# A decoder layer on one core: the first batch alone through its recurrence, context tiles behind the first heads, and four banks for the last product

## The chip, the cores and the metric

The kernel runs on one core of one Trainium2 chip. A core has TensorE (PE, the matrix engine, with its weight loads shown apart as PEld), VectorE (DVE), ScalarE (ACT), GpSimd (POOL) and SyncE (SP, which here only issues DMAs). Each engine works through its own instructions in order and waits on semaphores for the others. The metric is the device time of one execution in microseconds (us); a smaller number is better. Runs are compared by their median.

## The reference, cut to what matters

One decoder layer in 32-bit floats over x of shape (16, 256, 256), 16 batches of 256 tokens, with a context of 77 rows a batch:

```python
# 1. a recurrence over the tokens of each batch
h = x @ in_w.T + in_b                               # 512 channels
h = silu(depthwise_conv4(h) + conv_b)
xp = h @ xp_w.T + xp_b                              # 32 columns
a = exp(-exp(xp[..., :16]));  b = silu(xp[..., 16:]) * sum(h, -1)
state_t = state_{t-1} * a_t + b_t
x = layernorm(x + states @ out_w.T + out_b)
# 2. attention of the 256 tokens (as latents) over 77 context rows and themselves
xn = layernorm(ctx) * g_media + b_media;  ln = layernorm(x) * g_lat + b_lat
q = ln @ Wq + bq;  k, v = split(concat([xn, ln]) @ Wkv + bkv)   # 8 heads of 128
x = layernorm(x + softmax(q k / sqrt(128)) v @ Wo + bo)
# 3. eight experts, top 2 by token, at most 512 tokens each
x = layernorm(x + experts(x))
```

## The kernel before, in words

**Stages.** The kernel has an opening, a loop over 128 heads (16 batches of 8), and an expert part. The loop over heads is a software pipeline: for each head `head_kq` makes keys and queries (pk, pq), `head_softmax` the scores s, their maximum nm, the exponentials p and the normalised pn, `head_turn` the transposes ptt one head later, `head_out` the product po two heads later. Other work is hung on heads: `steps[b, h]`, filled by `at(...)`, runs after the head's keys and queries; `late_steps`, filled by `behind(...)`, after its transposes.

**The recurrence.** `rec_in(pr, c)` does one of four chunks of 128 channels for a pair of batches (512 tokens): two matmuls into a bank ph (L290), ACT copies it with the bias into hp (L293), whose first three columns POOL clears (L292, a buffer pair `bufs=2`), DVE makes the convolution cv in four instructions (L297, L299), ACT a tanh (L302) and DVE the activation hs (L303). For later pairs POOL sums hs over the chunks (L305). `rec_state` makes px and the sums sg by matmuls whose results take 32 partitions for each member (L319, L331); for the first pair its two members stand twice in the 128 partitions. Then come zb (L339), the decays on ACT (L341, L342), a permuting matmul pp (L344), and on DVE bs and the scan ys (L347 to L351). `rec_add` multiplies ys by the output weights (py, L363) and adds x (L369); `rec_out` normalises (L148, with a power on POOL, L134), `prep_norm` scales to zl (L425), `prep_keys` transposes zl and writes kvt (L437, L439), and `prep_values` makes v in seven products (L477) with weight sums wsum, which `weight_sums` makes on DVE (L448 to L451).

**The context.** The 16 x 77 context rows are ten tiles of 128 rows. `context(t)` normalises a tile, transposes it (pt, L389), writes kvc (L391), multiplies by the V half of wkv in two halves of two matmuls (pvc, L405), copies them out (DVE L413, ACT L415) and stores them to DRAM (L416), from where `prep_values` reads each batch's 77 rows. In the opening all ten tiles are called: 0 and 1 between the chunks, 2 to 4 between the steps of the first pair, and 5 to 9 after the values of batch 0.

**Banks.** PSUM has two banks "mm", which rotate between most users, one each of "pk", "pq", "pa" and "po", and a pair "s". The context's pvc use pk, pq, pa and po in turn.

**What sets the order.** A layer below the kernel orders each engine's instructions when the program is built, from the order in which the code calls them and its own estimate of their costs; the order on each engine is then fixed. Loads go out on two queues, SP's and ACT's, in the order of issue, and eight semaphores are used in turn for them: an issue waits until the earlier DMA with the same semaphore has landed.

**The last expert.** `second_product` multiplies four slots of 128 rows (pf, L996) into the two "mm" banks; for the last expert DVE adds each with its weight to y (L1004), where the gathered other halves (L985) are already added, and `finish` normalises and scatters.

Of the kernel before, what the change touches and what calls it, by code (L numbers as in the profile page):

```python
# [38 lines left out]
def decoder_layer(  # L39
# [152 lines left out]
    def load_xT(pr):  # L192

        xTs[pr] = aw.tile([P, DC, PT], F32, tag="xT", name=f"xT{pr}")
        nc.sync.dma_start(xTs[pr], xT[:, pr * PT : (pr + 1) * PT].rearrange("(c p) t -> p c t", p=P))
# [9 lines left out]
    nc.sync.dma_start(inw, in_wT.rearrange("(c p) f -> p c f", p=P))  # L205
    load_xT(0)
    for dst, src in ((inb, in_b), (cw, conv_w), (cb, conv_b), (gm, g_media), (bm, b_media)):
        nc.scalar.dma_start(dst, src)
    NCT = -(-B * M // P)

# [3 lines left out]
    ctx_flat = ctx_in.rearrange("b m d -> (b m) d")  # L214
    ctxs = []
    for t0, t1 in ((0, 1), (1, 5), (5, NCT - 1), (NCT - 1, NCT)):
        c = b2.tile([P, t1 - t0, D], F32, tag="v" if t1 - t0 == 4 else "ctx", name=f"ctx{t0}")
        rows = ctx_rows(t0)
        nc.sync.dma_start(
            c[0:rows, 0 : t1 - t0, :], ctx_flat[t0 * P : t0 * P + rows * (t1 - t0), :].rearrange("(t p) d -> p t d", p=rows)  # L220
        )
        ctxs += [c[:, i, :] for i in range(t1 - t0)]

    xpw = aw.tile([P, NI, 2 * NST], F32, tag="xpw", name="xpw")
    nc.sync.dma_start(xpw, xp_wT.rearrange("(c p) s -> p c s", p=P))
    half = aw.tile([P, 2 * NST], F32, tag="half", name="half")
    G.memset(half, 0.5)
# [4 lines left out]
    for g in range(0, P, 2 * NST):  # L232
        nc.sync.dma_start(xpb[g : g + 2 * NST], xp_b)
        nc.sync.dma_start(outw[g : g + NST], out_wT)
        nc.sync.dma_start(outw[g + NST : g + NST + 1], out_b)
# [7 lines left out]
    wkv_d = wkv.rearrange("(c p) f -> p c f", p=P)  # L243
    nc.sync.dma_start(wkv_s[:, :, INNER:], wkv_d[:, :, INNER:])
    load_x(0)
    load_x(1)
    for dst, src in ((gl, g_lat), (bl, b_lat), (bq_s, bq), (bkv_s, bkv)):
        nc.sync.dma_start(dst, src)
    nc.sync.dma_start(wkv_s[:, :, 0:INNER], wkv_d[:, :, 0:INNER])
    nc.sync.dma_start(wq_s, wq.rearrange("(c p) f -> p c f", p=P))  # L250
# [7 lines left out]
    def load_rest():  # L258
        nc.sync.dma_start(wo_s, wo.rearrange("(h p) f -> p h f", p=P))
        nc.sync.dma_start(bo_s, bo.broadcast_to([P, D]))  # L260
        nc.sync.dma_start(emb_s, embT.rearrange("(c p) e -> p c e", p=P))
    zero = wpool.tile([P, DX], F32, tag="zero", name="zero")
# [17 lines left out]
    hss, sums, yss, xs, stats = {}, {}, {}, {}, {}  # L280

    def rec_in(pr, c):

        if c == 0:
            hss[pr] = aw.tile([P, NI, PT], F32, tag="hs", bufs=2, name=f"hs{pr}")
            if pr > 0:
                sums[pr] = aw.tile([P, PT], F32, tag="sums", bufs=2, name=f"sums{pr}")
        ph = bank(f"ph{pr}_{c}")
        for k in range(DC):
            T.matmul(ph, lhsT=inw[:, k, c * P : (c + 1) * P], rhs=xTs[pr][:, k, :], start=(k == 0), stop=(k == DC - 1))  # L290
        hp = a2.tile([P, PB, KC - 1 + S], F32, tag="hp", name=f"hp{pr}_{c}")
        G.memset(hp[:, :, 0 : KC - 1], 0.0)  # L292
        A.activation(  # L293
            hp[:, :, KC - 1 :], ph.rearrange("p (b s) -> p b s", b=PB), AF.Identity, bias=inb[:, c : c + 1]
        )
        cv = a2.tile([P, PB, S], F32, tag="cv", name=f"cv{pr}_{c}")
        V.tensor_scalar(cv, hp[:, :, 0:S], cw[:, c, 0:1], cb[:, c : c + 1], ALU.mult, ALU.add)  # L297
        for k in range(1, KC):
            V.scalar_tensor_tensor(cv, hp[:, :, k : k + S], cw[:, c, k : k + 1], cv, ALU.mult, ALU.add)  # L299
        z = cv.rearrange("p b s -> p (b s)")  # L300
        th = a2.tile([P, PT], F32, tag="th", name=f"th{pr}_{c}")
        A.activation(th, z, AF.Tanh)  # L302
        V.scalar_tensor_tensor(hss[pr][:, c, :], th, 1.0, z, ALU.add, ALU.mult)  # L303
        if c > 0 and pr > 0:
            G.tensor_tensor(sums[pr], hss[pr][:, 0, :] if c == 1 else sums[pr], hss[pr][:, c, :], ALU.add)  # L305

    def rec_state(first, last):

        n = last - first + 1
        members = [first + g % n for g in range(4)]  # L310
        rows = [slice(g * 2 * NST, (g + 1) * 2 * NST) for g in range(4)]

        def tokens(b):
            return slice(b % PB * S, (b % PB + 1) * S)

        px = bank(f"px{first}")
        for c in range(NI):
            for b, r in zip(members, rows):
                T.matmul(  # L319
                    px[r, 0:S],  # L320
                    lhsT=xpw[:, c, :],
                    rhs=hss[b // PB][:, c, tokens(b)],
                    start=(c == 0),
                    stop=(c == NI - 1),
                )

        sg = bank(f"sg{first}")
        parts = [sums[b // PB] for b in members] if first else None
        for c in range(1 if first else NI):
            for g, (b, r) in enumerate(zip(members, rows)):  # L330
                T.matmul(  # L331
                    sg[r, 0:S],
                    lhsT=half,
                    rhs=parts[g][:, tokens(b)] if first else hss[0][:, c, tokens(b)],
                    start=(c == 0),
                    stop=(first > 0 or c == NI - 1),
                )
        zb = aw.tile([P, S], F32, tag="zb", name=f"zb{first}")
        V.tensor_scalar(zb, px[:, 0:S], xpb, None, ALU.add)  # L339
        dec = aw.tile([P, S], F32, tag="dec", name=f"dec{first}")  # L340
        A.activation(dec, zb, AF.Exp)  # L341
        A.activation(dec, dec, AF.Exp, scale=-1.0)  # L342
        pp = bank(f"pp{first}")
        T.matmul(pp[:, 0:S], lhsT=perm, rhs=zb, start=True, stop=True)  # L344
        bs = aw.tile([P, S], F32, tag="bs", name=f"bs{first}")
        A.activation(bs, pp[:, 0:S], AF.Tanh, scale=0.5)
        V.scalar_tensor_tensor(bs, bs, 1.0, pp[:, 0:S], ALU.add, ALU.mult)  # L347
        V.tensor_tensor(bs, bs, sg[:, 0:S], ALU.mult)
        ys = a2.tile([P, S], F32, tag="ys", name=f"ys{first}")
        V.tensor_tensor_scan(ys, dec, bs, 0.0, ALU.mult, ALU.add)  # L350
        V.tensor_scalar(ys, ys, one_row, None, ALU.add)  # L351
        for b, r in zip(members[0:n], rows):
            yss[b] = ys[r, :], outw[r, :]
# [3 lines left out]
    def rec_add(b):  # L357

        pys = [bank(f"py{b + i}") for i in range(PB)]
        for h in range(2):  # L360
            for i in range(PB):
                ys, w = yss[b + i]
                T.matmul(  # L363
                    pys[i][:, h * D : (h + 1) * D], lhsT=ys[:, h * P : (h + 1) * P], rhs=w, start=True, stop=True
                )
        for i in range(PB):
# [15 lines left out]
    def context(t):  # L382
# [3 lines left out]
        layernorm(zc, zc, 1, rows, f"c{t}")  # L386
        pt = bank(f"pt{t}")
# [10 lines left out]
        if t % 2 == 0:  # L398
            stages[t // 2] = b2.tile([P, 2, INNER], F32, tag="ot", name=f"vc{t}")
        vc = stages[t // 2][:, t % 2, :]  # L400
        for half in range(2):
            f0 = half * 512
            pv = bank(f"pvc{t}_{half}", ("pk", "pq", "pa", "po")[(2 * t + half) % 4], 1)
# [8 lines left out]
            if half == 0:  # L412
                V.tensor_copy(vc[0:rows, f0 : f0 + 512], pv[0:rows])  # L413
            else:
                A.copy(vc[0:rows, f0 : f0 + 512], pv[0:rows])  # L415
        nc.sync.dma_start(vc_d[t * P : t * P + rows, :], vc[0:rows, :])  # L416
# [27 lines left out]
    def weight_sums():  # L444
# [3 lines left out]
        V.tensor_tensor(t(0), w(0, 1), w(0, 0), ALU.subtract)  # L448
        V.tensor_tensor(t(1), w(1, 1), w(0, 1), ALU.subtract)
        V.tensor_tensor(t(2), w(1, 1), t(0), ALU.subtract)  # L450
        V.tensor_tensor(t(3), w(1, 0), t(2), ALU.subtract)  # L451
# [328 lines left out]

    for h in range(H):
        at(0, h, clear, h)
    at(1, 0, clear, H)
    for b in range(B):
# [11 lines left out]
        if new_pair:  # L796
# [4 lines left out]
            at(b, 1, rec_add, nb)  # L801
# [5 lines left out]
            for n, h in enumerate((4, 6, 7)):  # L807
                at(b, h, prep_values, nb, n, False)
                behind(b, h, prep_values, nb, n, True)
        elif nb < B:  # L810
# [7 lines left out]
    at(0, 0, load_xT, 1)  # L818
    for c in range(NI):
        at(0, 4 + c, rec_in, 1, c)  # L820
    for nb in range(4, B, 4):
# [6 lines left out]
        for c, h in enumerate((3, 4, 5, 7)):  # L828
            at(nb - 2, h, rec_in, pr + 1, c)

    rec_in(0, 0)
    rec_in(0, 1)
    context(0)
    rec_in(0, 2)
    rec_in(0, 3)
    context(1)
    rec_state(0, 1)
    context(2)
    context(3)
    rec_add(0)  # L840
    rec_out(0)
    prep_norm(0)
    prep_keys(0)
    context(4)
    rec_out(1)
# [5 lines left out]
    for t in range(5, NCT):  # L851
        context(t)
# [134 lines left out]
    def second_product(e, it):  # L987
# [5 lines left out]
        for s in range(SLOTS[e][2]):  # L993
            po = bank(f"pf{e}_{s}")
# [184 lines left out]
```

## Time and profile before

| what | us |
|---|---|
| median of 3 runs | 1200.22 (1199.39 to 1200.71) |
| the profiled execution | 1201.09 |
| its span, first to last instruction | 1199.3 |
| PE busy in the span | 1152.6 (96%) |
| DVE busy | 748.6 (62%) |
| ACT busy | 485.4 (40%) |
| POOL busy | 312.3 (26%) |

The page says how long each engine was busy, in 40 slices of the span and as groups of instructions by line. A line of the timeline gives start, time, engine, line, operation, what is written and read, and in brackets how long the engine was idle before it and what ended that. Engine time that overlaps other work does not add to the span, so the shares of busy time do not by themselves say what sets the end.

### The profile page before, as it was taken

The numbers are of one execution on the slowest core, as the hardware profiler recorded it, in microseconds if no ns is written. First come the engines' busy times: TensorE is split into PE (matmuls) and PEld (weight loads), VectorE is DVE, ScalarE is ACT, GpSimd is POOL, SyncE is SP. The second block draws the span as 40 slices with busy tenths as digits, with TensorE's granted clock in tenths as the row PEclk, the third lists the DMA queues.
The fourth block names the chain that finished last, engine by engine and source line by source line (L and its number), as shares of the span: only waits on it lengthen the run. The fifth ranks groups of instructions, "written<-read, shape, count | busy, mean of one in ns | idle before, by whom it ended". The sixth has DMA issues, their size and how long they took to land. (4 is left out here: it accounts for less than half of the span.)

```text
span 1199.3 us, 15750 instructions
## 1 busy us (share of the span) xinstructions
PE 1152.6 (96%) x5134; PEld 827.8 (69%) x5134; DVE 748.6 (62%) x2226; ACT 485.4 (40%) x1273; POOL 312.3 (26%) x560
## 2 busy tenths in 40 slices
PE   6789999999999999999999999999999999999996
PEld 2337676767777767767777777677777778876664
DVE  5535768596646765874658576756465645666665
ACT  2125434444344434443435343534343433423331
POOL 2200132222221332222213222232122211225554
PEclk8899999999999999999999999999999999999999
DMA  6760001001000110010000000010001000125762
GB/s 207 226 188 11 19 20 37 28 10 56 18 29 9 35 36 23 9 46 18 15 10 23 29 21 9 4 29 4 20 14 45 14 9 3 30 92 171 182 182 85
DMA packets 45402, 60.37 MB, mean 50 GB/s; under 512 B 7813, under 2 KB 35438, under 8 KB 45320
## 3 DMA queue, kind: packets, MB, share of 16 engines
q1 hardware_dynamic: 38552, 50.13, 13.6%
q0 software_dynamic: 6048, 9.22, 3.1%
q8 instruction: 41, 0.67, 0.2%
q14 instruction: 41, 0.34, 0.1%
q10 hardware_dynamic: 720, 0.01, 0.0%
HBM read 36.07 MB, written 30.78 MB: 56 GB/s over the span
## 5 line engine op out<-in xcount | busy, mean ns | idle before, releaser
L564 PE MATMUL po<-ptt,v 128*128 128x256 f32 (+1 forms) x768 | 190.0, 382 | 6.3 <-DVE ptt L552 6.3
L564 PEld LDWEIGHTS po<-ptt,v 128*128 128x128 f32 (+1 forms) x768 | 142.7, 190 | 58.7 <-issue 25.7
L529 DVE TENSOR_REDUCE nm<-s 128x2 f32<-128x666 f32 x128 | 108.3, 846 | 117.1 <-PE s L527 117.1
L512 PE MATMUL pk<-kvt,wkv_s 128*128 128x333 f32 x512 | 164.9, 444 | 0.0
L527 PE MATMUL s<-kt,qt 128*128 128x333 f32 x512 | 164.3, 442 | 0.0
L572 ACT ACTIVATE ot<-po,bkv_s 128x256 f32<-128x256 f32 x128 | 60.8, 475 | 218.9 <-PE po L564 218.7
L533 ACT ACTIVATE p<-s,nm 128x333 f32<-128x333 f32 x256 | 135.4, 535 | 33.7 <-DVE nm L529 32.5
L517 PE MATMUL pq<-kvt,wq_s 128*128 128x256 f32 x512 | 131.2, 378 | 0.0
L512 PEld LDWEIGHTS pk<-kvt,wkv_s 128*128 128x128 f32 x512 | 91.1, 191 | 45.0 <-issue 22.0
L527 PEld LDWEIGHTS s<-kt,qt 128*128 128x128 f32 x512 | 96.4, 188 | 31.3 <-ACT qt L519 0.5
L517 PEld LDWEIGHTS pq<-kvt,wq_s 128*128 128x128 f32 x512 | 96.7, 189 | 30.2
L582 PE MATMUL pw<-wo_s,ot 128*128 128x256 f32 x512 | 115.8, 379 | 0.0
L553 ACT COPY ptt<-pb 77x256 f32<-77x256 f32 x128 | 47.1, 368 | 168.2 <-PE pb L550 168.2
L582 PEld LDWEIGHTS pw<-wo_s,ot 128*128 128x128 f32 x512 | 97.0, 190 | 13.2
L538 DVE TENSOR_SCALAR pn<-p,rs 128x333 f32<-128x333 f32 x256 | 97.8, 416 | 3.8
L760 POOL DMA_INDIRECT xg<-xs,sidx x64 | 66.4, 1038 | 88.7 <-DVE sidx L757 68.0
L550 PEld LDWEIGHTS pa<-ident,pn 128*128 128x128 f32 x512 | 63.6, 141 | 34.8 <-DVE pn L538 6.8
L552 DVE COPY ptt<-pa 128x512 f32<-128x512 f32 x128 | 87.1, 680 | 0.6 <-PE pa L550 0.6
L596 POOL TENSOR_TENSOR xb<-xs,bo_s 128x256 f32<-128x256 f32 x30 | 19.9, 683 | 244.1 <-DVE yb L598 244.1
L550 PE MATMUL pa<-ident,pn 128*128 128x128 f32 x512 | 78.3, 274 | 2.6 <-DVE pn L538 2.6
L514 ACT ACTIVATE kt<-pk,bkv_s 128x333 f32<-128x333 f32 x128 | 69.0, 539 | 19.9 <-PE pk L512 19.6
L299 DVE SCALAR_TENSOR_TENSOR cv<-hp,cw,cv 128x512 f32<-128x512 f32 x96 | 71.8, 751 | 1.9
(231 smaller groups left out, 1670.0 us busy)
## 6 DMA issues: line engine op xcount, KB each, us to landing
v<-vc SPq DMA_DIRECT2D x16, 308.0 KB
vc<-vc SPq DMA_DIRECT2D x9, 512.0 KB
xg<-zero SPq DMA_DIRECT2D x34, 131.0 KB
xe<-xg SPq DMA_DIRECT2D x8, 524.0 KB
xT<-in_xT SPq DMA_DIRECT2D x8, 512.0 KB
xt<-in_x_in SPq DMA_DIRECT2D x16, 256.0 KB
out<-o SPq DMA_DIRECT2D x16, 256.0 KB
w<-in_w1T SPq DMA_DIRECT2D x8, 512.0 KB
```

Of the source, the lines that this page charges most:

```text
L299: V.scalar_tensor_tensor(cv, hp[:, :, k : k + S], cw[:, c, k : k + 1], cv, ALU.mult, ALU.add)
L512: T.matmul(pk[:, 0:J], lhsT=wkv_s[:, k, f], rhs=kvt[:, k, :], start=(k == 0), stop=(k == DC - 1))
L514: A.activation(kt, pk[:, 0:J], AF.Identity, bias=bkv_s[:, h : h + 1])
L517: T.matmul(pq[:, 0:S], lhsT=wq_s[:, k, f], rhs=kvt[:, k, 0:S], start=(k == 0), stop=(k == DC - 1))
L527: T.matmul(s[:, ic, 0:J], lhsT=qt[:, ic * P : (ic + 1) * P], rhs=kt, start=True, stop=True)
L529: V.tensor_reduce(nm, s[:, :, 0:J], AX.X, ALU.max, negate=True)
L533: A.activation(p[:, ic, :], s[:, ic, 0:J], AF.Exp, bias=nm[:, ic : ic + 1], accum_out=sm[:, ic : ic + 1])
L538: V.tensor_scalar(pn[:, ic, :], p[:, ic, :], rs[:, ic : ic + 1], None, ALU.mult)
L550: T.transpose(dst[0:jn, c0 : c0 + P], pn[:, ic, j0 : j0 + jn], ident)
L552: turned = V.tensor_copy(ptt[:, 0:2, :], pt01.rearrange("p (j i) -> p j i", j=2))
L564: T.matmul(po[:, 0:S], lhsT=vs[b][0:jn, jc, h * DH : (h + 1) * DH], rhs=ptt[0:jn, jc, :], start=(jc == 0), stop=(jc == 2),)
L582: T.matmul(pws[b][:, i * D : (i + 1) * D], lhsT=ot[:, h, i * P : (i + 1) * P], rhs=wo_s[:, h, :], start=(h == 0), stop=(h == H - 1),)
```

## The change

- `load_xT` and `rec_in` can take one batch of the first pair; before the heads only batch 0 goes through the recurrence (256 columns, one member in `rec_state`, which now repeats no members). Batch 1's chunks are called at heads 0 and 1, its `rec_state` at head 2, `rec_add` and `rec_out` at head 3, keys at head 4, values at heads 5, 6 and 7.
- The context is split: five tiles are normalised together (`context_norm`) and called between the steps of batch 0; tiles 5 to 9 run behind heads 0 to 4, with pt and pvc in the "mm" banks and each half stored by itself. The middle tiles are loaded into the second hs buffer; the first tiles' pt take the "s" pair.
- The loads are issued in another order: half of xT, inw in two halves, the first five tiles and the V half of wkv come first; the recurrence's small weights go to ACT's queue, and their copies for the other members after the opening.
- The four weight sums go from DVE to POOL.
- The chunks of the second pair of each four batches are called at heads 2, 3, 5, 6 instead of 3, 4, 5, 7.
- The last expert's third and fourth slots of `second_product` take the banks "pk" and "pq".

```diff
+    load_xT(0, 0)
+    nc.sync.dma_start(inw[:, :, 0 : DI // 2], inw_d[:, :, 0 : DI // 2])
+    nc.sync.dma_start(inw[:, :, DI // 2 :], inw_d[:, :, DI // 2 :])
+    load_ctx(ctx_ends[0], 0, 1)
+    load_ctx(ctx_most, 1, 5)
+    nc.sync.dma_start(wkv_s[:, :, INNER:], wkv_d[:, :, INNER:])
...
+    load_x(0)
+    nc.sync.dma_start(gl, g_lat)
+    nc.sync.dma_start(bl, b_lat)
+    nc.sync.dma_start(wkv_s[:, :, 0:INNER], wkv_d[:, :, 0:INNER])
...
+    def rec_in(pr, c, i=None):
+        a, n = (0, PB) if i is None else (i, 1)
+        cols = slice(a * S, (a + n) * S)
+        ph = bank(f"ph{pr}_{c}")[:, 0 : n * S]
...
     def rec_state(first, last):
-        n = last - first + 1
-        members = [first + g % n for g in range(4)]
+        members = range(first, last + 1)
...
+    def context_norm(t):
+        zc = ctxs[t].unsqueeze(1)
+        layernorm(zc, zc, 1, ctx_rows(t), f"c{t}")
...
+    def context(t, first):
+        if not first:
+            context_norm(t)
+        if first:
+            pt = ps.tile([P, 2, 512], F32, tag="s", bufs=1, name=f"pt{t}")[:, t % 2, :]
+        else:
+            pt = bank(f"pt{t}")
...
+            if first:
...
+                pv = bank(f"pvc{t}_{half}", ("pk", "pq", "pa", "po")[(2 * t + half) % 4], 1)
+            else:
+                vc = b1.tile([P, 512], F32, tag=("xb", "x2")[half], name=f"vc{t}_{half}")
+                pv = bank(f"pvc{t}_{half}")
...
-        V.tensor_tensor(t(0), w(0, 1), w(0, 0), ALU.subtract)
+        G.tensor_tensor(t(0), w(0, 1), w(0, 0), ALU.subtract)
...
+        elif b == 0:
+            for h in range(2):
+                at(0, h, rec_in, 0, 2 * h, 1)
+                at(0, h, rec_in, 0, 2 * h + 1, 1)
+            at(0, 2, load_xT, 1)
+            at(0, 2, rec_state, 1, 1)
+            at(0, 3, rec_add, 1, 1)
+            at(0, 3, rec_out, 1)
+            at(0, 4, prep_norm, 1)
+            at(0, 4, prep_keys, 1)
+            at(0, 4, prep_sums, 1)
+            for n, h in enumerate((5, 6, 7)):
+                at(0, h, prep_values, 1, n, False)
+                behind(0, h, prep_values, 1, n, True)
+            for h in range(NCT - FIRST_CTX):
+                behind(0, h, context, FIRST_CTX + h, False)
...
-        for c, h in enumerate((3, 4, 5, 7)):
+        for c, h in enumerate((2, 3, 5, 6)):
             at(nb - 2, h, rec_in, pr + 1, c)
...
+    for c in range(NI):
+        rec_in(0, c, 0)
+    for t in range(FIRST_CTX):
+        context_norm(t)
+    context(0, True)
+    rec_state(0, 0)
+    context(1, True)
+    rec_add(0, 1)
+    context(2, True)
     rec_out(0)
     prep_norm(0)
+    context(3, True)
     prep_keys(0)
-    context(4)
-    rec_out(1)
+    context(4, True)
     wparts = weight_sums()
     prep_sums(0)
...
-    for t in range(5, NCT):
-        context(t)
...
-            po = bank(f"pf{e}_{s}")
+            po = bank(f"pf{e}_{s}") if e < LAST or s < 2 else bank(f"pf{e}_{s}", ("pk", "pq")[s - 2], 1)
```

## The prediction

> **What bounds the kernel now.** I read the page's slices first, then the busy time by stretches of 10 us, then TensorE's timeline of the opening, then the waits of the DMA queue. The slices and stretches say that there are two regimes.
>
> ```profile
> PE   6789999999999999999999999999999999999996
> 20.00:30.00 10.00, 9.54 (x23) 3.71 (x24) 7.01 (x12) 2.79 (x5) 0.95 (x3) 0.66 0.45 181
> 40.00:50.00 10.00, 5.67 (x19) 2.39 (x17) 4.81 (x16) 1.17 (x2) 1.18 (x4) 0.89 0.64 209
> 50.00:60.00 10.00, 6.83 (x14) 3.18 (x15) 6.04 (x22) 0.81 (x2) 7.55 (x19) 0.60 0.74 215
> 100.00:110.00 10.00, 10.00 (x49) 7.91 (x49) 4.25 (x10) 5.16 (x15) 0.00 (x0) 1.00 0.00 0
> ```
>
> Columns of a stretch: length, busy time of PE, its weight loads, DVE, ACT, POOL, then the granted clock. From about 90 us on TensorE is full, so a microsecond of its work costs a microsecond. Before that it is not: over 0 to 90 us the stretches sum to 67.6 us busy, 22.4 idle, and twice the clock is down (0.66, 0.60). The timeline shows what the idle time waits for.
>
> ```profile
> 6.26 5.66 PE L290 MATMUL ph<-xT,inw 128*128 128x512 f32 x8 [6.26 <-DMA xT<-in_xT]
> 21.99 9.78 PE L405 MATMUL pvc<-wkv_s,kvc 128*128 128x512 f32 x16
> 37.47 7.13 PE L405 MATMUL pvc<-wkv_s,kvc 128*128 128x512 f32 x16
> 44.54 1.13 PE L363 MATMUL py<-outw,ys 32*128 32x256 f32 x8
> 52.18 1.45 PE L437 MATMUL pt<-ident,zl 128*128 128x128 f32 x4 [6.51 <-DVE zl L425]
> 82.41 7.13 PE L405 MATMUL pvc<-wkv_s,kvc 128*128 128x512 f32 x16 [0.68 <-ACT kvc L391]
> 89.38 1.28 PE L512 MATMUL pk<-kvt,wkv_s 128*128 128x333 f32 x4
> ```
>
> The first batch's recurrence is one chain: ph, convolution on DVE (from 13.49 us, last hs at 31.98), zb 33.27, ys ready 38.07, py only at 44.54 because context tiles 2 and 3 stand ahead of it in TensorE's queue, the add at 45.70, zl done at about 52, kvt at 55.2. The first head (pk) starts at 89.38, after five more context tiles.
>
> **The loads.** TensorE's start halves its operands: before, 1 MB (inw and xT) had to land, and the DMAs moved 391 GB/s from 3 to 5 us. After, 0.5 MB is enough: 0.5/0.391 = 1.3 us earlier, 4.9 instead of 6.26. But the queue that issues loads waits for semaphores of earlier, tiny loads:
>
> ```profile
> SPq L219 <- DMA inb<-in_in_b: 2.0, 1, 2.0
> SPq L219 <- DMA cw<-in_conv_w: 0.6, 1, 0.6
> SPq L225 <- DMA cb<-in_conv_b: 0.6, 1, 0.6
> ```
>
> inb landed at 4.31, cw at 5.86, cb at 6.78. The waits of the changed program put the same three ahead of other loads: context tile 0 behind inb, tiles 1 to 4 behind cw, the V half of wkv behind cb. Before, tiles 1 to 4 were issued at 4.31 and read at 8.35, 4.0 us later. Issued at 5.5 to 5.9 with less ahead of them, I put them at 9.2 (3.5 after 5.7), and V, issued at 6.5, at 11.9 (2 us before bytes flow, 1 MB at 0.39 is 2.6, 0.8 until seen). Before, V was issued at 12.67.
>
> **The chain of batch 0.** In DVE's new order the statistics of five context tiles stand ahead of the first convolution: two tiles and small operations took 8.35 to 9.64 (1.29), two more add 2 x 0.37 and aggregates, together 2.4: convolution from 11.6 instead of 13.49. It is 256 wide, not 512: about 0.33 and three times 0.41 a chunk (a 128x256 operation of this kind, bs, takes 0.42; the 512 ones 0.75) plus 0.4 for hs. The third chunk's hp buffer needs a memset on POOL, and there the weight sums now come first. Their price:
>
> ```profile
> L305 POOL TENSOR_TENSOR sums<-sums,hs x14: 1276/1285/1355, 136.0 to 771.3; 128x512 f32<-128x512 f32 x14
> L448 DVE TENSOR_TENSOR wsum<-wkv_s x1: 684/684/684, 27.7 to 27.7; 128x512 f32<-128x512 f32 x1
> ```
>
> Four sums of 1.3 and a kvt copy of 0.6 from V's landing: 12.0 + 5.8 = 17.9. DVE would be there at 15.7, so moving four times 0.68 off it costs the chain a wait of 2.2. From 17.9 the rest of the convolution, two normalisations, a PSUM copy and hs are 6.1: last hs at 24.0 (before 31.98). zb follows 1.7 later, 25.7. To ys the old distance holds (33.27 to 38.07, 4.8): 30.5. py now stands after half a tile only: add at 31.7 (before 45.70). Add to zl was 6.2 with two batches interleaved; one batch with three context statistics in between I take at 6.0: 37.7. TensorE, given the tiles left behind py (0.9 + 1.8 + 0.4 + 0.7 of wait + 3.6 from 30.6), is free for the transposes at 38. kvt follows at 39 to 40. Then context tile 4 (16 of the 128x512 take 7.13, so 3.6 a tile) and the seven V products (0.86 each, one ahead of tile 4), 1 us of bank waits: **pk at 51**, against 89.38: 38.4 earlier.
>
> **What moves behind the heads** and costs its full time there: tiles 5 to 9, 3.57 + 0.43 each, 20.0; rec_in of batch 1, four chunks of four matmuls of 256 columns at 0.223, 3.6; its py 0.6; its px, sg and pp. For these:
>
> ```profile
> 142.01 1.99 PE L319 MATMUL px<-hs,xpw 128*32 128x256 f32 x32
> ```
>
> The row gives 62 ns an instruction, so 16 of px and sg would be 1.0. The Trainium skill (TensorEngine Tiling (Array Packing), "Theoretical Speedup" and "Key Properties") says that up to four tiles with 32 columns work side by side; the row was four members side by side, and one member uses one tile. By the rule its 16 take 16 x 4 x 0.062 = 4.0. I take the rule, plus 0.2 for pp: 4.2. No run of before has one member alone. For batch 0 this stands in the chain's idle time. Sum moved: 20.0 + 3.6 + 0.6 + 4.2 = **28.4**. Net of the opening: 38.4 - 28.4 = **10.0 faster**.
>
> **The clock.** The low grants of 20 to 30 and 50 to 60 us made 16 matmuls 9.78 instead of 7.13 and tile 4's eight about 5.1 instead of 3.6. The skill (TensorE: Matmul & The Clock Gate, Part 1) says half speed comes after an idle window of about 3.4 us. My new gaps are 9.6 to 12 and 16.7 to 19, each under that: by the rule no loss. By the row, the first low grant came at 20.7 with no gap over 2.2 us since 16.4, only light use; so one dip, worth 1.5 to 2.7 of TensorE's time, is possible. Nothing on the chain waits for TensorE there except px, so I count half a microsecond, inside the 51.
>
> **New stalls in the heads.** Each tile's three banks and each chunk's one rotate through the two "mm" banks, and are freed by DVE copies and ACT reads. In heads 0 and 1 DVE has 0.85 of reduce, 0.7 of pn, 0.68 of ptt, 0.69 of tile copy and two chunks of 2.0, 6.9 together; TensorE has 5.06 (pk at 99.26 to pk at 104.32), 4.0 of tile and 1.8 of chunks, 10.9. What can stall is DVE standing on a POOL rsqrt with a copy behind it; the trace has such cases:
>
> ```profile
> 181.89 1.54 PE L564 MATMUL po<-ptt,v 128*128 128x256 f32 x6 [1.24 <-DVE ptt L552]
> 278.18 0.63 PE L331 MATMUL sg<-sums,half 128*32 128x256 f32 x4 [0.75 <-POOL sums L305]
> ```
>
> Tiles 8 and 9 and the output normalisation of batch 1 come in the heads; tiles 5 to 7 are normalised before. Bounds: 0, and 1.24 at each of five heads, 6; nearest is one or two such cases, **1.5 lost**. The loads (xT of pair 1, the vc stores, v) have 15 us or more to land; if xT were late, its chunk at head 4 would stall by what it is late.
>
> **Elsewhere.** Pairs' chunks at heads 2, 3, 5, 6 in place of 3, 4, 5, 7 end the three sg waits (0.75, 0.68, 0.68: 2.1); the chunk at 6 meets the expert choice on DVE. Bounds -2.1 and +1; **1.0 gained**. The last product in four banks:
>
> ```profile
> 1187.28 3.72 PE L996 MATMUL pf<-w,it 128*128 128x256 f32 x16 [1.79 <-DVE ye L1004]
> 1189.70 0.47 DVE L1004 SCALAR_TENSOR_TENSOR ye<-pf,we,ye 128x256 f32<-128x256 f32 x1
> 1191.47 0.47 DVE L1004 SCALAR_TENSOR_TENSOR ye<-pf,we,ye 128x256 f32<-128x256 f32 x1
> ```
>
> TensorE waits for the first two banks, but pf of slots 2 and 3 are done at about 1189.1 and 1191.0, before DVE, in an unchanged order, reaches them at 1189.70 and 1191.47. Cover: DVE's own chain. **0** (0.3 at most).
>
> **Sum.** 10.0 - 1.5 + 1.0 = 9.5. Span 1199.3 - 9.5 = 1189.8. The profiled run took 1201.09 (1.8 around the span), 0.87 over the median of 1200.22; so I forecast a median of 1200.22 - 9.5 = **1190.7**.
>
> **Rivals.** (1) The chain isn't shortened that much: POOL blocks it. If V lands 4 us later (its issue waits for cb), the memset and all behind it come 4 us later and pk is at 55; with stalls of 3: gain 38.4 - 4 - 28.4 - 3 + 1 = 4: 1196. For it: the three queue waits above; against: less bulk lies ahead of inb, cw and cb than before, so they should land no later. (2) The heads cover everything, and zl comes at 34 because POOL's sums don't hold DVE up: pk at 47, no stalls: gain 15, 1185. For it: DVE has time in the heads; against: POOL runs in order. (3) Slower: the tiles in the heads starve the two "mm" banks. In the opening tiles use four other banks; in the heads each tile takes three turns of two banks which DVE frees in order behind reduce, convolution and rsqrt waits. It decides where a head loses over 1.5 us more at all of eight heads, 12 in sum; the longest such loss in the trace is 1.24, once, so this needs what no stretch shows: loss 18, 1208. (4) It does nothing: the same price at 1.1 a head over eight heads eats 9; 1200.
>
> **How the numbers follow.** Forecast case 0.69 (1187 to 1194.5), rival 1 0.14, rival 2 0.07, rival 3 0.06, rival 4 0.04. Three runs of before span 0.11%, so 0.2% (2.4 us) is about what can be told from no change. Faster: forecast, rivals 1 and 2: 0.90; same 0.04; slower 0.06. Range: the forecast case widened by V's landing and the head stalls upward, by the uncovered POOL wait downward: 1186 to 1197 holds the forecast case and rival 1, and leaves out rivals 2, 3 and 4 (0.17).
>
> **What would show it.** pk's first matmul near 51 (under 47 or over 55 refutes the chain); first convolution at 11 to 12; a DVE wait for POOL ahead of the third chunk of about 2; add of batch 0 near 32; one-member px and sg taking about 4 in all; TensorE idle in the first eight heads under 3; no sg wait on sums at the three later pairs; the tail from the last gather unchanged. The prediction is wrong if the heads' period grows beyond their TensorE work, or a load holds the chain.

## The result, and the profile after

The changed kernel took 1192.04 us (median of four runs, 1191.17 to 1193.58) against 1199.81 for the kernel before beside it (four runs): 7.8 us less, a ratio of 0.9937 with a 95% interval of 0.992 to 0.9954. The forecast was 1190.7 in a range of 1186 to 1197. A later set of runs gave only 1.3 us, and that has a section of its own under the experiments.

The profiled execution took 1192.6, its span 1190.9 (before 1201.09 and 1199.3). First the page's line of busy times and TensorE's slices, then the busy time by stretches of 10 us (length; busy time of PE, weight loads, DVE, ACT, POOL; granted clock; DMA).

```profile
PE 1155.1 (97%) x5100; PEld 830.7 (70%) x5100; DVE 754.0 (63%) x2247; ACT 487.5 (41%) x1284; POOL 317.7 (27%) x568
PE   6899999999999999999999999999999999999996
```

```profile
20.00:30.00 10.00, 9.69 (x28) 3.41 (x26) 7.01 (x22) 3.23 (x9) 1.85 (x5) 0.87 0.26 85
40.00:50.00 10.00, 7.93 (x20) 3.68 (x19) 3.23 (x8) 2.56 (x5) 2.55 (x6) 0.83 0.18 61
50.00:60.00 10.00, 9.99 (x34) 5.74 (x33) 5.11 (x10) 2.62 (x6) 0.00 (x0) 1.00 0.97 260
```

TensorE does as much as before (1155.1 us busy against 1152.6), but is full from 50 us on where it was full from 90. The clock still falls twice, shorter than before (0.87 and 0.83 where it was 0.66 and 0.60).

TensorE's timeline of the opening and of the first heads (start, length, what; in brackets how long it stood and for whom):

```profile
4.75 4.93 PE L321 MATMUL ph<-xT,inw 128*128 128x256 f32 x12 [4.75 <-DMA inw<-in_in_wT]
...
31.56 1.13 PE L401 MATMUL py<-outw,ys 32*128 32x256 f32 x4
...
42.92 1.88 PE L531 MATMUL pv<-wkv_s,kvt 128*128 128x512 f32 x2 [2.07 <-DVE kvt L493]
44.59 4.58 PE L456 MATMUL pvc<-wkv_s,kvc 128*128 128x512 f32 x8
...
54.67 1.28 PE L566 MATMUL pk<-kvt,wkv_s 128*128 128x333 f32 x4
...
74.99 1.91 PE L357 MATMUL px<-hs,xpw 128*32 128x256 f32 x8
76.74 1.89 PE L369 MATMUL sg<-hs,half 128*32 128x256 f32 x8
...
136.33 1.92 PE L357 MATMUL px<-hs,xpw 128*32 128x256 f32 x16
```

The first head starts at 54.67 instead of 89.38: the opening is 34.7 shorter (forecast 38.4). From the first pk to px of the second pair it is 81.66 us instead of 52.63 (142.01 less 89.38): 29.0 moved behind the heads (forecast 28.4, and 1.5 of stalls). That leaves 5.7. Up to the last pk of the loop another 1.9 is gained (1036.91 against 1044.45 is 7.5), and behind it 0.9 in the experts, together the 8.4 of the spans.

TensorE's waits between 60 and 1060 us (total, times, longest):

```profile
PE po L618 <- DVE ptt L606: 7.5, 10, 1.3
PE pa L604 <- DVE pn L592: 2.7, 5, 0.5
PE ph L321 <- ACT v L550: 0.4, 1, 0.4
PE pt L436 <- DVE ctx L148: 0.4, 1, 0.4
```

The tiles behind the heads cost one stall of 0.4 in all (pt for ctx). The waits of sg for POOL's sums, 2.9 in four cases before, are gone; po's wait for ptt grew from 6.3 in seven cases to 7.5 in ten.

### The profile page after: what moved, and what is told of

Read it like the earlier page. It is cut to its first block, busy times and chain, and to the rows that moved or that the text cites. A ratio compares the mean times of both kernels' runs of the same rounds, so it can differ in the third digit from the quotient of the medians.

```text
span 1190.9 us, 15723 instructions
## 1 busy us (share of the span) xinstructions
PE 1155.1 (97%) x5100; PEld 830.7 (70%) x5100; DVE 754.0 (63%) x2247; ACT 487.5 (41%) x1284; POOL 317.7 (27%) x568
## 5 line engine op out<-in xcount | busy, mean ns | idle before, releaser
L571 PEld LDWEIGHTS pq<-kvt,wq_s 128*128 128x128 f32 x512 | 96.7, 189 | 30.5 <-issue 0.5
L336 DVE SCALAR_TENSOR_TENSOR cv<-hp,cw,cv 128x512 f32<-128x512 f32 (+1 forms) x108 | 76.8, 719 | 1.6
```

Source lines behind the costliest of these rows:

```text
L571: T.matmul(pq[:, 0:S], lhsT=wq_s[:, k, f], rhs=kvt[:, k, 0:S], start=(k == 0), stop=(k == DC - 1))
```

## The experiments

They ran in three sets, each on a chip of its own with the kernel before beside it. All times below are medians. The changed kernel stood in the first comparison, whose chip is not on record, and in set 3; a kernel of set 1 or 2 that is set against its 1192.04 may therefore be compared across chips, and a difference of a microsecond there decides nothing without the traces.

| kernel | set | us | ratio to before, 95% |
|---|---|---|---|
| weight sums on DVE | 1 | 1187.58 | 0.9881 to 0.993 |
| third and fourth hp in other buffers | 1 | 1193.53 | 0.9934 to 0.9968 |
| all ten tiles in the opening | 1 | 1191.59 | 0.9916 to 0.995 |
| first pair, not one batch, in the opening | 1 | 1196.66 | 0.9958 to 0.9983 |
| sums on DVE, tiles 5 to 9 normalised behind kvt | 2 | 1187.08 | 0.9876 to 0.9911 |
| tiles 5 to 9 normalised behind kvt | 2 | 1190.13 | 0.9903 to 0.9934 |
| later pairs at heads 3, 4, 5, 7 | 2 | 1194.06 | 0.9933 to 0.9967 |
| last product in two banks | 2 | 1193.23 | 0.993 to 0.9965 |
| the changed kernel again | 3 | 1199.80 | 0.9979 to 0.9999 |
| sums on DVE again | 3 | 1195.05 | 0.994 to 0.9969 |
| sums on DVE, tiles behind kvt again | 3 | 1192.97 | 0.9915 to 0.9941 |
| the same, convolution first | 3 | 1190.81 | 0.9895 to 0.9924 |

Before took 1199.98, 1199.33 and 1201.12 in the three sets.

### What holds the convolution: a wait for POOL, or its company

The forecast had DVE wait 2.2 us for hp's memset, which stands behind the four weight sums on POOL. The profile after shows no such wait. It shows DVE's convolution steps slow while POOL adds. DVE and POOL of the changed kernel, then the busy time of that stretch (as above, all five engines):

```profile
11.88 4.75 DVE L336 SCALAR_TENSOR_TENSOR cv<-hp,cw,cv 128x256 f32<-128x256 f32 x4
16.56 1.35 DVE L148 TENSOR_SCALAR ctx<-ctx,mvc,rc 128x256 f32<-128x256 f32 x1
...
20.26 1.26 DVE L336 SCALAR_TENSOR_TENSOR cv<-hp,cw,cv 128x256 f32<-128x256 f32 x3
```

```profile
11.60 1.49 POOL L502 TENSOR_TENSOR wsum<-wkv_s 128x512 f32<-128x512 f32 x1 [0.30 <-DMA wkv_s<-in_wkv]
13.05 1.45 POOL L503 TENSOR_TENSOR wsum<-wkv_s 128x512 f32<-128x512 f32 x1
```

```profile
11.60:17.80 6.20, 4.44 (x14) 2.04 (x12) 6.20 (x7) 1.59 (x4) 6.12 (x6) 1.00 1.03 365
```

Four steps in 4.75 us, then three in 1.26: beside POOL's sums a step takes up to 1.49 us instead of 0.47, and DVE gets about as many instructions done (seven) as POOL (six). DVE counts as busy all the while; nothing in the waits tells of it. A normalisation with one tile as its input (1.35 instead of 0.41) is stretched as well. Two kernels tell the explanations apart.

The first has the sums on DVE again:

```diff
-        G.tensor_tensor(t(0), w(0, 1), w(0, 0), ALU.subtract)
+        V.tensor_tensor(t(0), w(0, 1), w(0, 0), ALU.subtract)
```

(and the other three alike)

> The changed kernel with the four weight sums on DVE again. Two theories of why DVE is slow from 11.6 to 17.8 us. Port: a DVE operation with two SBUF inputs and a two-input POOL operation take turns, so each convolution step lasts as long as the sum beside it (1.49 instead of 0.47). Then the convolution steps are back at 0.47, the last hs ends about 3.8 us earlier (at 20.7), two sums of 0.68 stand before zb and two in a wait: the chain is 2.4 us shorter, pk at 52.3, time about 1189.6. Queue (the prediction's step): DVE is held only by the hp memset behind POOL's sums. Then the memset's wait of 2.2 goes and 1.4 to 2.7 of DVE work comes: -0.8 to +0.5, about 1192, and the steps before the third chunk stay slow.

The second has hp of batch 0's third and fourth chunk in buffers of their own, so that no memset waits for a chunk before it:

```diff
-        hp = a2.tile([P, PB, KC - 1 + S], F32, tag="hp", name=f"hp{pr}_{c}")[:, 0:n]
+        if i == 0 and c > 1:
+            hp = aw.tile([P, PT], F32, tag="sums", bufs=2, name=f"hp{pr}_{c}")[:, 0 : KC - 1 + S].unsqueeze(1)
+        else:
+            hp = a2.tile([P, PB, KC - 1 + S], F32, tag="hp", name=f"hp{pr}_{c}")[:, 0:n]
```

> The changed kernel with buffers of their own for the third and fourth chunk's hp of batch 0, so that POOL's memsets stand ahead of its sums; the sums stay on POOL. Queue theory: DVE no longer waits for the memset, the last hs comes 2.2 us earlier, time about 1189.8. Port theory: DVE's convolution steps are still 1.3 to 1.5 beside the sums; the last hs moves by less than 0.7 and the time by less than 1.

The convolution's steps by the operations that write and read cv, with the sums on DVE (count: shortest, median, longest in ns):

```profile
L336 DVE SCALAR_TENSOR_TENSOR cv<-hp,cw,cv x12: 478/482/486, 12.3 to 19.5; 128x256 f32<-128x256 f32 x12
```

and with hp in other buffers (below it four of these steps in the timeline):

```profile
L339 DVE SCALAR_TENSOR_TENSOR cv<-hp,cw,cv x108: 473/748/1486, 12.3 to 756.0; 128x512 f32<-128x512 f32 x84, 128x256 f32<-128x256 f32 x24
...
14.01 4.75 DVE L339 SCALAR_TENSOR_TENSOR cv<-hp,cw,cv 128x256 f32<-128x256 f32 x4
```

Without POOL's sums every one of the twelve steps takes 0.48; with them, and no buffer to wait for, four steps still take 4.75 and the longest 1.486. From the first convolution to the last hs it is 13.60 us in the changed kernel, 13.43 with hp in other buffers and 9.40 with the sums on DVE. The time says the same: 1187.58 against 1193.53 on one chip. The wait for POOL's queue is refuted; the company on POOL is shown to be the cause. The loads are not: with the sums on DVE the DMA engines' share was 0.96 from 12.3 to 19.5 us, and the steps were short. The gain of the sums on DVE, 4.5 us, was more than expected: the last hs came at 21.02 instead of 24.12 (3.1, though the convolution began 1.1 later), and the low clock of 43 to 47 us did not return.

### Tiles behind the heads

All of tiles 5 to 9 back in the opening, with the rest of the change kept:

```diff
-            for h in range(NCT - FIRST_CTX):
-                behind(0, h, context, FIRST_CTX + h, False)
...
+    for t in range(FIRST_CTX, NCT):
+        context_norm(t)
+        context(t, True)
```

> The changed kernel with context tiles 5 to 9 in the opening, after the values of batch 0, as before the change; the rest as changed. My theory: TensorE is full either way, so moving the tiles is worth only the waits for kvc that they had in the opening (0.6 at each of three pairs) less what they cost in the heads (0.4): +1 to +2, about 1193.5; pk at about 75. Rival: the moved tiles are the gain, so without the move the time is back within 2 of the kernel before, 1198 or more.

1191.59 us, 0.5 under the changed kernel's 1192.04 with overlapping runs. The first head starts 17.5 later, and that costs nothing in the end:

```profile
42.14 3.70 PE L456 MATMUL pvc<-wkv_s,kvc 128*128 128x512 f32 x8 [0.55 <-ACT kvc L438]
45.67 1.02 PE L531 MATMUL pv<-wkv_s,kvt 128*128 128x512 f32 x2
...
72.17 1.33 PE L566 MATMUL pk<-kvt,wkv_s 128*128 128x333 f32 x4
```

But the edit does more than move five tiles. In the order that was built for it tile 4's pvc stands ahead of the first pv, so TensorE does not wait for kvt (2.07 in the changed kernel), though kvt comes at 44.05, and no low clock follows. That hides what the tiles are worth. From py to px of the second pair TensorE takes 104.77 us in the changed kernel and 102.71 here, but 101.41 in a kernel below (tiles 5 to 9 normalised behind kvt), which keeps the tiles behind the heads and loses the wait in another way. With the wait gone in both, the tiles behind the heads are worth 1.3, as expected (1 to 2), by one profile of each on two chips; the times, 1191.59 and 1190.13, differ by 1.5. Most of what the opening loses the heads take at the same price.

### One batch or two in the opening

Both batches of the first pair go through the recurrence before the heads, as in the kernel before. The tiles and the sums stay as changed; the loads that the second batch needs (its half of xT, its x and small weights) come forward with it, so TensorE starts at 5.87 instead of 4.75:

```diff
-        rec_in(0, c, 0)
+        rec_in(0, c)
...
-    rec_state(0, 0)
+    rec_state(0, 1)
...
-    rec_add(0, 1)
+    rec_add(0, 2)
...
+    rec_out(1)
```

> The changed kernel with both batches of the first pair through the recurrence together, 512 columns wide, as before; the tiles behind the heads, the loads, the sums on POOL and the order of py as changed. My theory: DVE's convolution is twice as long (7 to 8 us), additions and normalisations 2 more, so pk comes at 62 to 65, but 8.4 us of TensorE work leave the heads: 0 to +2, 1192 to 1194. Rival: the single batch carries the gain, and with the pair the time is back at 1198 or more; or it costs, and the time is 1188 or less, because the one-member matmuls and the second pass cost more than they save.

1196.66 us, 4.6 slower than the changed kernel, more than the 0 to 2 that were expected. The recurrence's last hs came at 36.74 instead of 24.12, and the first pk at

```profile
68.18 1.28 PE L566 MATMUL pk<-kvt,wkv_s 128*128 128x333 f32 x4
```

13.5 later. Of that 9.8 is made up behind it: from the first pk to px of the second pair it is 71.86 us instead of 81.66, for batch 1's work no longer stands in the heads. At the last pk of the loop this kernel is 4.8 behind (1041.72 against 1036.91). The clock stood at half for 17.1 us of its opening, in the changed kernel for 6.8. So of the 7.8 us gained the single batch, with its smaller first load, carries about 4.6; the rest comes with the other parts.

### What kvt stands behind, and the clock

In the changed kernel TensorE waits 2.07 for kvt, because in DVE's queue the normalisation of tiles 5 to 7, which waits for POOL's rsqrt, stands ahead of the kvt copies. The next edit holds it behind them:

```diff
+            with tc.issue_after(keys[0].ins):
+                context_norm(t)
-            context_norm(t)
...
-            V.tensor_scalar(
+            keys[b] = V.tensor_scalar(
```

> Only the second of those edits: the sums stay on POOL, the normalisation of context tiles 5 to 9 is held behind the first kvt copies. My theory: kvt (42.33 in the changed kernel) comes about 2 earlier, near 40.3; TensorE's wait of 2.07 goes, and with it the low grant of 43 to 47 us (about 1.9 of TensorE's time), so pk is near 51 and the time 1188.3 (between a gain of 2.0 if the clock still falls and 3.9 if it does not). Rival A (POOL's operations of tiles 5 to 7 are not what kvt stands behind): pk within 0.5 of 54.67 and 1192. Rival B (the low grant follows from the light use before it, not from the gap): kvt earlier by 2, but 16 matmuls of pvc near 45 us still take more than 8 us, and 1190.

1190.13 us where 1188.3 was expected, 1.9 under the changed kernel's first 1192.04 and 3.1 under the nearest kernel of its own set, 1193.23 (two banks, below). Its opening reached py at 32.83, 1.27 later than the changed kernel, before anything that differs; from py to the first pk it took 19.76 instead of 23.11. The wait fell to

```profile
PE pv L532 <- DVE kvt L494: 0.4, 1, 0.4
```

and no low grant followed: 3.35 us gained from py, near the theory's upper figure of 3.9. Rival A and rival B are refuted by this trace (pk at 52.59, eight pvc in 3.60); the time alone would have fitted rival B.

The same edit on top of the sums on DVE:

> Two edits on the changed kernel: the four weight sums of the opening on DVE again, and the normalisation of context tiles 5 to 9 held behind the first kvt copies in DVE's order. My theory (with the sums on DVE, kvt came at 39.07 us because DVE stood in front of it for POOL's rc of tiles 5 to 7, and TensorE idled 2.05 for it): kvt near 37, that wait under 0.5, pk near 47.7 instead of 49.72, 1185.6 us against the 1187.58 of the sums on DVE alone. Rival A (the wait only moves: TensorE, the V products or the bank copies set pk): pk within 0.5 of 49.7 and 1187.6. Rival B (the later normalisation is late for tile 5 in the first head): pk near 47.7, but a new wait of TensorE for ctx in the heads and 1187 or more.

1187.08 us. py to pk fell from 21.40 (49.72 less 28.32, sums on DVE alone) to 19.76 (49.28 less 29.52), 1.64, but this opening too ran 1.2 later, and pk moved only from 49.72 to 49.28. Against the 1187.58 of the other chip the time shows no gain. In the third set both ran on one chip:

> The sums on DVE once more, beside the changed kernel: if the DVE steps that shared their time with POOL were worth what the traces say (last hs 3.1 earlier, and no low grant behind kvt), it is 4.5 us faster than the changed kernel again, 1188.0. Rival (the first comparison caught a good run): 2 us faster or less.

> The sums on DVE and the normalisation of tiles 5 to 9 behind the first kvt copies once more. Its first opening ran 1.2 later than that of the sums alone (py at 29.52 against 28.32), before anything that differs; measured from py, pk came 1.64 earlier (19.76 against 21.40). My theory: that 1.6 shows in the time, 1186.4 against 1188.0 here. Rival: no difference, within 0.5.

The sums on DVE gained 4.75 against the changed kernel (1195.05 against 1199.80), as first. The two edits together gained 2.1 more (1192.97). From py to pk it was again 1.65 (21.42 and 19.77); yet pk came only 0.43 earlier, for in both profiles of the two edits a low clock fell between 11 and 16 us, and the convolution took 10.53 and 10.56 to its last hs instead of 9.40. So the 1.65 is shown in the trace; the 2.1 of time fits but is more than pk explains.

Why did the gap of 2.07 bring a low clock in the changed kernel, and a gap of 2.05 none with the sums on DVE? The busy time by stretches of 3.41 us, laid on the steps of the granted clock (PE alone, then clock and DMA), of the changed kernel:

```profile
15.86:19.27 3.41, 0.77 (x3) 1.00 1.04 371
19.27:22.68 3.41, 3.01 (x8) 0.50 0.28 89
39.75:43.16 3.41, 1.34 (x9) 1.00 0.37 134
43.16:46.57 3.41, 3.41 (x5) 0.50 0.16 50
```

and with the sums on DVE:

```profile
37.95:41.36 3.41, 1.70 (x4) 1.00 0.44 164
41.36:44.77 3.41, 3.41 (x9) 1.00 0.03 5
```

The clock changes only between such stretches, and each fall goes with the stretch before: 0.77 and 1.34 busy were followed by half the clock, 1.70 by the full one. The same held wherever the clock was full in the first 70 us of all fourteen profiles: 17 stretches with 0.77 to 1.36 busy were followed by a half, every one with 1.58 or more by full. The same gap may thus fall into one stretch or be split between two. Five profiles have the changed kernel's order at this place: in four the gap fell into one stretch (1.34 to 1.36 busy, then half), in the one with hp in other buffers it was split over two (2.29 and 2.49 busy, full). With the sums on DVE it was split in both (1.70 and 1.59 in the emptier stretch). Whether that place is chance, or follows from the opening, is open.

### The convolution ahead of the tiles' statistics

```diff
+            convs[pr, c] = V.scalar_tensor_tensor(cv, hp[:, :, k : k + S], cw[:, c, k : k + 1], cv, ALU.mult, ALU.add)
...
+    context_norm(0)
+    for t in range(1, FIRST_CTX):
+        with tc.issue_after(convs[0, 1].ins):
+            context_norm(t)
...
+    with tc.issue_after(convs[0, 3].ins):
+        wparts = weight_sums()
```

> On top of the kernel before it: the statistics of context tiles 1 to 4 are held behind the convolution's first two chunks in DVE's order, and the weight sums behind its last. This tests the step of my working that puts the convolution at 11.6 because five tiles' statistics stand in front of it. My theory: DVE stood 2.2 to 2.6 for the DMA of tiles 1 to 4 while hp was ready at 7.5; the convolution starts near 7.6 instead of 11.5, the last hs comes 2.5 to 3 earlier, pk 2.5 earlier, 1183.9 us. Rival A (TensorE's fourth ph stands behind the first tile's transposes, or px behind pvc, whose weights land at 11.6): last hs 1 earlier at most, pk within 1, 1186. Rival B (the tiles' later statistics hold their transposes up): px early, but TensorE waits for ctx of tiles 1 to 4, pk no earlier or later, 1187.

1190.81 us beside 1192.97, 2.2 faster (2.5 expected; the ranges overlap), and 10.3 faster than the kernel before on that chip. The convolution starts at

```profile
7.70 0.41 DVE L334 TENSOR_SCALAR cv<-hp,cw,cb 128x256 f32<-128x256 f32 x1
```

instead of 10.73, the last hs at 17.46 instead of 21.26, the first pk at 46.54 instead of 48.47. So 3.8 at the hs, 3.1 at zb (20.63 and 23.73), 1.1 at py (27.63 and 28.70). About 1.1 of the 3.8 is the low clock of 11 to 15 us, which this profile did not have. What is lost between zb and py is lost on DVE: the weight sums, put off until after the convolution, now stand between the steps of bs, the scan and ys.

```profile
24.77 0.67 DVE L505 TENSOR_TENSOR wsum<-wkv_s,wsum 128x512 f32<-128x512 f32 x1
25.37 0.67 DVE L388 TENSOR_TENSOR_SCAN ys<-dec,bs 32x256 f32<-32x256 f32 x1
25.97 0.65 DVE L506 TENSOR_TENSOR wsum<-wkv_s,wsum 128x512 f32<-128x512 f32 x1
```

From zb to the last step of ys it takes 5.92 us instead of 3.96; from there to py 1.08 and 1.01. Rival A (pk within 1) and rival B (pk no earlier) are both refuted; pk gained 1.9 where 2.5 was expected.

### Two parts alone

The chunks of the later pairs at the old heads:

```diff
-        for c, h in enumerate((2, 3, 5, 6)):
+        for c, h in enumerate((3, 4, 5, 7)):
```

> Undoes one part: the input chunks of the later pairs stand at heads 3, 4, 5 and 7 again instead of 2, 3, 5 and 6. What I forecast for this part: 1.0 lost when it is undone, 1193.0 us, with waits of sg for POOL's sums of 0.7 each at the three later pairs (2.1) back, and about 1.2 less of po waiting for ptt. Rival: the waits only change places, and the time stays within 0.3 of 1192.0.

The last product in two banks:

```diff
-            po = bank(f"pf{e}_{s}") if e < LAST or s < 2 else bank(f"pf{e}_{s}", ("pk", "pq")[s - 2], 1)
+            po = bank(f"pf{e}_{s}")
```

> Undoes one part: the last product takes turns of two banks again instead of four banks. What I forecast: no change (0, at most 0.3): TensorE's wait of 1.8 for DVE's ye is back in the last product, while DVE's own chain from the last gather to the last output stays at 7.7 us; 1192.0. Rival (the four banks are worth the wait that they end): 1193.8.

They took 1194.06 and 1193.23, with ranges that overlap. The traces decide more sharply. With the old heads the waits that TensorE had before are back:

```profile
PE po L618 <- DVE ptt L606: 6.3, 7, 1.3
...
PE sg L369 <- POOL sums L343: 2.0, 3, 0.7
```

2.0 more for sg and 1.2 less for po, net 0.8; the times differ by 0.8. From px of the second pair to the last pk it is 1.6 more than with two banks (902.03 against 900.44), so the heads moved are worth 0.8 to 1.6, near the 1.0 forecast. With two banks TensorE waits again in the tail,

```profile
1179.45 3.72 PE L1063 MATMUL pf<-w,it 128*128 128x256 f32 x16 [1.02 <-DVE ye L1071]
```

but DVE's chain, from the last gathered half (1178.51) to the start of the last output (1186.22), takes 7.71, and with four banks 7.72 (1177.88 to 1185.60). The four banks are worth nothing. The median of 1193.23 lies nearer to the rival's 1193.8 than to 1192.0, but in this profile the opening already ran 0.86 later, before anything that differs (py at 32.42).

### The changed kernel in the third set

> The changed kernel unaltered, beside the three below. What it settles: whether the low grant of 43 to 47 us comes back behind the gap of 2.07 (my theory: yes, the 16 matmuls of pvc from about 45 us take over 4 us and pk is 23.0 us behind py; rival: the grant differs from run to run and pk is 21.5 behind py), and what the others are worth beside it. 1192.5 us.

The gap and the low clock came back as expected: py to pk took 23.11 again. The time did not: 1199.80 against 1201.12 for the kernel before, 1.3 us gained, where the first comparison had 7.8. The two intervals do not meet, and 1199.80 lies outside the forecast's range. The profile of this run has a span of 1199.8, 8.9 over that of the first. Beside the first profile, the opening is 0.43 later; three times, at 273 to 279, 520 to 526 and 766 to 772 us, 1.55 is lost; and 3.9 between 1115 us and the end, among the experts. TensorE's waits there:

```profile
PE pp L382 <- issue: 3.9, 3, 1.3
PE pf L1063 <- ACT ye L1073: 3.0, 2, 1.6
```

The three losses are of one kind. POOL and DVE near the first one, in this run,

```profile
273.24 0.97 POOL L814 DMA_INDIRECT xg<-xs,sidx  x1 [0.30 <-issue]
274.05 0.48 DVE L377 TENSOR_SCALAR zb<-px,xpb 128x256 f32<-128x256 f32 x1 [2.57 <-PE po L618]
274.51 0.97 POOL L814 DMA_INDIRECT xg<-xs,sidx  x1 [0.31 <-issue]
```

in the first profile of the changed kernel,

```profile
271.53 0.97 POOL L814 DMA_INDIRECT xg<-xs,sidx  x1 [0.30 <-issue]
271.88 0.48 DVE L377 TENSOR_SCALAR zb<-px,xpb 128x256 f32<-128x256 f32 x1 [0.83 <-PE px L357]
272.81 0.98 POOL L814 DMA_INDIRECT xg<-xs,sidx  x1 [0.30 <-issue]
```

and in the kernel before.

```profile
274.61 1.11 POOL L760 DMA_INDIRECT xg<-xs,sidx  x1 [0.30 <-issue]
277.43 0.48 DVE L339 TENSOR_SCALAR zb<-px,xpb 128x256 f32<-128x256 f32 x1 [0.42 <-PE px L319]
```

px has finished at 272.2, yet zb, which waits for it, starts at 274.05, in the midst of POOL's four scatters; pp and the heads stand behind it. In the first profile zb starts as soon as px is done, also between scatters. In the kernel before, and with the later pairs at the old heads, zb comes after the fourth scatter: heads 2, 3, 5, 6 moved it between them. All four kernels of the third set have these three waits (3.8 to 3.9 in all), no profile of the other two sets or of the first comparison has. That the scatters delay the signal from TensorE on that chip is argued from the places where they meet, not shown: the old heads did not run on that chip, and the kernel before has no profile from it. Why the experts lose up to 3.9 there is open, and so is whether the chip itself or something else in that set is the cause. The gain of the sums on DVE was the same as before, 4.75 and 4.5.

## Why the prediction was right, and where it was wrong

**Loads.** TensorE's start (4.9) was right: 4.75. The three queue waits ahead of the loads came where they were put, 2.6 in sum against 3.2 before. Tiles 1 to 4 were read at 8.39 where I put 9.2; the V half by 11.60 where I put 11.9. The convolution therefore began at 10.52, not 11.6. This profile is the earliest of its kind: in ten others whose first convolution is ordered alike, it began at 10.73 to 11.69, near the forecast.

```profile
SPq L218 <- DMA inb<-in_in_b: 1.3, 1, 1.3
...
SPq L234 <- DMA cb<-in_conv_b: 0.8, 1, 0.8
...
SPq L218 <- DMA cw<-in_conv_w: 0.5, 1, 0.5
```

**The step that failed: "moving four times 0.68 off it costs the chain a wait of 2.2"**, a wait of DVE for the memset behind POOL's sums. There was no such wait. DVE's own steps were stretched, five of them (four of the convolution, one normalisation) from 11.88 to 17.83, 5.95 us for what takes 1.9 with the sums on DVE (12.99 to 14.90): 4.0 lost, not 2.2. The last hs came at 24.12 against 24.0 only because the earlier start and the larger loss cancelled, and that was luck. The Trainium skill (SBUF — State Buffer, "SBUF: two separate sides") says that VectorE and GpSimd take an exclusive lock on a shared port pair, held for the whole instruction, by VectorE for an operation with two SBUF inputs among others; 1.49 of a step beside 1.49 of a sum looks like taking turns. That rule would have spoken against the move to POOL from the start; I had not weighed it. The lock itself was not measured apart; the company was. And the turns are not complete: 0.47 and 1.28 one after the other would make 1.75 a pair.

**zb to zl** was right within a microsecond or so: zb 26.48 (25.7), ys 30.86 to its end (30.5), the add 32.72 (31.7), zl 39.0 (37.7).

**Mis-sized: "kvt follows at 39 to 40".** It came at 42.33, because the normalisation of tiles 5 to 7 and its waits for POOL stand between zl and kvt. The text named that tiles 5 to 7 are normalised before the heads, and priced neither their place in DVE's queue nor their rsqrt: 2.07 of TensorE's time, confirmed by holding them back.

**Mis-sized: the clock.** Half a microsecond was counted; the second low grant made two pv 1.88 instead of 1.12 and eight pvc 4.58 instead of 3.60, 1.7 in sum; py to pk says the same, 23.11 against 21.40 with hp in other buffers, where the gap was as long and the clock stayed full. Between the row (a fall after light use, 1.5 to 2.7) and the rule as I read it (a whole idle stretch of 3.4 us, no loss), the row was right. The Trainium skill (TensorE: Matmul & The Clock Gate, Part 1) also says that the stretches run free of the kernel, which agrees with the steps of 3.41 us and with gaps that are hit or missed. The runs add that a stretch need not be idle: up to 1.36 of 3.41 busy was still followed by half.

These two, 3.35 together by the kernel that took both away, are most of why pk came at 54.67 and not at 51. The forecast named a pk over 55 as the sign that its chain was wrong. 54.67 is just under it, and three later profiles with the same opening had pk at 55.10 to 55.52.

**Moved work.** 29.0 measured against 28.4 and 1.5 of head stalls: the stalls were 0.4. px and sg of one member took 1.91 and 1.89, 3.8: the 4.0 estimated by the tiling rule was right, and the 1.0 that the row's mean would have given was wrong. For two members px took 1.92 as well.

**Elsewhere.** The sg waits ended as said, po's grew by 1.2, which the step had not in it; the sum, 1.7 or so net in the first comparison, was more than the 1.0 forecast because the fourth sg wait, at 144.79 us, fell too; with the old heads three sg waits came back and not this one, so it belongs to another part. The four banks: nothing, as said.

**The sum** was 9.5 and the gain 7.8: the opening gained 3.7 less than forecast, the moved work cost 0.9 less with its stalls, and behind that 1.7 more was gained than the 1.0 put there. That makes the 8.4 of the spans; the medians show 7.8. Rival 1 (POOL holds the chain, pk at 55) had the place of pk right for another reason; V was not late. Rival 3 (the tiles starve the two "mm" banks) found no sign: one stall of 0.4. No case of the forecast held a loss that comes with the chip or the set; in the third set the changed kernel came out near rival 4's 1200, from another cause than rival 4's.

## What to carry to other kernels

Before moving an elementwise operation to GpSimd because VectorE is on the path, ask what VectorE does at that moment: beside it, its two-input steps took three times as long while both counted as busy, so that a move which takes 2.7 us off VectorE cost 4.5. When TensorE is full, moving its work from one stage to another is worth little by itself (1.3 for 20 us of tiles); what counts is idle time that it fills, and that is found by asking what the first dependent instruction (here kvt) stands behind in its engine's queue. And a gain of half a per cent is not settled by one set on one chip: measure a second before it is believed.

## What the runs showed of the hardware

- VectorE's 128x256 two-input step took 0.47 alone and up to 1.49 beside GpSimd's 128x512 sums (1.32 to 1.49 each; 1.28 for such a sum in the heads of the kernel before). Both engines counted as busy.
- TensorE's clock changed only between stretches of 3.41 us, whose place differed from run to run; from the full clock, stretches with 1.36 us of matmuls or less were followed by half of it, those with 1.58 or more were not (fourteen profiles, first 70 us).
- px of one member (8 matmuls of 256 columns, 32 wide) took 1.91 us, of two (16 matmuls) 1.92, and of four (32) 1.99 in the kernel before.
- The same program took 1192.04 us in one set and 1199.80 in another, while the kernel before differed by 1.3. Of the 8.9 by which the two spans differ, 4.65 stands at three places where VectorE's zb falls among GpSimd's indirect scatters (at the first, 1.8 us after px had ended); 3.9 among the experts is unexplained.
